# Moving one addition from VectorE to GpSimd, five transposes to a later place, and two sums ahead of two transfers, in a two-way cross-attention kernel

## The chip, the cores and the metric

The kernel runs on one core of a Trainium2 chip. The metric is the device time of one execution in microseconds (us); three executions of the kernel before gave 942.03, 942.37 and 944.33 us, with a median of 942.37. Engines are named as in the profile: PE is TensorE (PEld its weight loads), DVE is VectorE, ACT is ScalarE, POOL is GpSimd, SP is the queue that starts most transfers. "L12" is line 12 of the kernel before.

## The reference, cut to what matters

All arrays are float32. There are B = 16 batches of S = 100 query rows of width H = 640, and a context of 722 tokens of width 384 for each batch. The last 4 tokens (`ca`) are split off; the other 718 (`enc`) are keys and values of an ordinary attention with 8 heads of width 80. The 4 tokens feed a second attention, whose queries come out of a third one over the rows of `x`. Both results are added and projected:

```python
hs = _mha(hidden_states @ Wq, enc @ Wk, enc @ Wv)
ca_q1 = jnp.einsum('btc,th->bch', ca, Wq_ca)[:, indices, :]
ca_q2 = _mha(ca_q1, residual, residual) @ Wq
ca_hs2 = _mha(ca_q2, ca @ Wk_ca, ca @ Wv_ca)
out = (hs + ca_hs2) @ Wout + b_out + residual
```

## The kernel before, in words

A preparation of about 60 us loads and combines weights and makes the keys and values of batch 0. Then a Python loop over the 16 batches `b` issues everything in an order that is written out by hand: each engine runs its own queue in exactly the order of the code, and engines wait for each other through semaphores only where data or buffers demand it. No scheduler moves anything in the loop.

One step of the loop, for the batches 1 to 14, goes like this:

- `scores` (L623): three groups of score matmuls for batch b; ACT copies them to `st[0..2]`, and DVE keeps a running maximum `most` (L1229). `Maximum` turns that into one maximum for each row, `top.over`, through two 32x32 transposes on DVE (L675, L705) and reductions.
- `Values` (L443) makes the values of batch b, and `Keys` (L474) the keys of batch b+1, by a fast matrix multiplication that needs 15 products each. A product accumulates in a PSUM bank (A to E) which is read several times, between products: by ACT the first time that a block of the result is touched (L416), by DVE as an addition later (L414). So PE may write a bank again only when the reading before it has ended. `vv.go(n)` and `kk.go(n)` issue the next n products; `both(n)` does both. Banks C, D and E come from a pool of two PSUM buffers (`psum1`), keys' A and B from another of two (`psumk`).
- Among these products stand `subtract(i)` on DVE (L1217, `st[i]` minus the maximum) and `exponential(i)` on ACT (L1225).
- The second attention is computed by element-wise work: `second.scores1` for batch b+1 (POOL, L784 and L791), `now.scores2` and `now.softmax3` for batch b (small DVE work; L862 makes the weights `p`), and `now.values2` (POOL, L876 products and L883 sums), which writes `hs2`. Its four input rows `vb` are transfers: two of them started from POOL's own queue by `load` (L833), two from SP.
- `last_keys` (L568) makes the last 128 columns of the keys of batch b+1. After odd batches `queries` (L544) makes the queries of the next two batches.
- The values are applied to the probabilities (L1409), and DVE writes `hs` (L1423). For all batches but 0, DVE also adds `hs2` there (L1430). In batch 0, `hs2` is not ready by then, and the addition is done later, in batch 1's step.
- `last` is the batch before. `last.transpose()` transposes its `hs` in five pieces of 128 columns on PE (L931) into one PSUM tile `hst_ps`, and ACT copies them to `hsT` (L944). In the batches from 2 on this stands at the start of the step.
- The output projection takes chunks of 128 rows. Ten of the thirteen chunks are done in five pairs (`PAIRS`, in the steps b = 3, 6, 8, 11 and 13) by `project_pair` (L1010), which saves products by using sums of the two chunks. `last.sums()` makes the first two sums on POOL (L991): `sum1`, and a new first part of `two = hsT[r+1]`. `project_pair` begins with five matmuls that need neither (b1 and b2), then come two that need the second sum and the combined weight `wout2`. POOL's own steps between are L1027, L1030 and L1031; L1030 overwrites what the two matmuls read, and L1031 makes the weight for a later product.

In batch 1's step before the change, the late addition (L1315) stands on DVE between four readings of PSUM banks and `top.go()` (L705), and the transposes of batch 0 stand among the products, into a `psum1` buffer.

Of the kernel before, what the change touches and what calls it, by code (L numbers as in the profile page):

```python
# [10 lines left out]
ALU = mybir.AluOpType  # L11
# [3 lines left out]
B, S, H = 16, 100, 640  # L15
# [4 lines left out]
HC = H // P  # L20
# [18 lines left out]
PAIRS = {ENDS[r + 1]: r for r in range(0, 10, 2)}  # L39
# [96 lines left out]
def kernel(  # L136
# [18 lines left out]
    nc = tc.nc  # L155
# [21 lines left out]
    def psumk(name):  # L177
        return psk.tile([P, 512], F32, tag="psk", name=name)
# [24 lines left out]
    def hsT_tile(name):  # L203
        return main.tile([P, HC, P], F32, tag="hsT", name=name, bufs=3)
# [19 lines left out]
    def rest_tile(name):  # L224
        return main.tile([P, len(A_REST), KT], F32, tag="rest", name=name)

    def load_enc(b):
        enc = enc_tile(f"enc_{b}"), None
        for u, lo, hi in ((0, 0, 3), (1, 1, 3), (2, 0, 2)):
            at = A_RAW[u, lo]  # L230
            nc.sync.dma_start(
                out=enc[0][:, at : at + hi - lo],
                in_=enct[b][:, lo:hi, u * (KT - 1) : u * (KT - 1) + KT],
            )
        return enc

    def load_rest(b, enc):
        if b == 1:
            room = hsT_tile("rest_1").rearrange("p c s -> p (c s)")
            rest = room[:, : len(A_REST) * KT].rearrange("p (i k) -> p i k", k=KT)  # L240
        else:
            rest = rest_tile(f"rest_{b}")
        for (u, c), i in A_REST.items():
            nc.sync.dma_start(
                out=rest[:, i], in_=enct[b][:, c, u * (KT - 1) : u * (KT - 1) + KT]
            )
        return enc[0], rest
# [459 lines left out]
    def load_m(b):  # L707
        if b < 2:
            return lambda c: m_sb[c][:, b * HT : (b + 1) * HT]
        mb = small.tile([P, HC, HT], F32, tag="mb", name=f"mb_{b}", bufs=2)  # L710
        nc.sync.dma_start(
            out=mb, in_=m_d[:, :, b * HT : (b + 1) * HT].rearrange("c p n -> p c n")
        )
        return lambda c: mb[:, c]
# [182 lines left out]
    class Last:  # L897
# [23 lines left out]
                return [(0, slice(0, H))]  # L921
            return [(64 * k, slice(k * (H // 2), (k + 1) * (H // 2))) for k in range(2)]

        def transpose(self, chunks=[(0, HC)], get=psumk):
            b, hs = self.b, self.hs
            if not self.t_ps:
                self.t_ps = get(f"hst_ps_{b}")
            t_v = self.t_ps[:, : HC * S].rearrange("p (c s) -> p c s", c=HC)
            for c0, c1 in chunks:
                for c in range(c0, c1):  # L930
                    nc.tensor.transpose(  # L931
                        t_v[:, c], hs[:S, c * P : (c + 1) * P], ident[:S, :S]
                    )
                for r, (lo, n) in enumerate(OC):
                    first, end = max(lo, b * S), min(lo + n, (b + 1) * S)
                    if first >= end:
                        continue
                    if r not in hsTs:
                        hsTs[r] = (
                            spare[0].rearrange("p (c s) -> p c s", c=HC)  # L940
                            if r == len(OC) - 1
                            else hsT_tile(f"hsT_{r}")
                        )
                    nc.scalar.copy(  # L944
                        hsTs[r][:, c0:c1, first - lo : end - lo],
                        t_v[:, c0:c1, first - b * S : end - b * S],
                    )
# [238 lines left out]
    last, enc_next, second_next = None, load_rest(1, load_enc(1)), Second(1, xT)  # L1186
# [8 lines left out]
    for b in range(B):  # L1195
# [28 lines left out]
        def exponential(i):  # L1224
            nc.scalar.activation(st[i], st[i], AF.Exp, scale=SCALE)  # L1225
# [29 lines left out]
        if b == 0:  # L1255
            second.scores1()
            m_next = load_m(b + 2)
            kk.go(3)
            top.go(3)
            first_values(3, e_in, (act, act), get=bank)  # L1260
            top.go(1)
            kk.go(2)
            now.scores2()
            first_values(0, e_in, (act, act), (0,), bank)
            top.go()
            kk.go(3)
            first_values(0, e_in, (act, act), (1,), bank)
            now.softmax3()
            kk.go(2)
            subtract(0)  # L1270
            exponential(0)
            kk.go(2)
            subtract(1)
            kk.go(3)
            exponential(1)
            second_next, enc_next = loads()
            less = subtract(2)
            exponential(2)
            last_keys(b + 1, enc)
            enc_next = load_rest(b + 2, enc_next)  # L1280
            keys(m_next)
            now.values2(less)
            enc_sums(enc_next)
            second.softmax1(4)
        elif b + 1 < B:
            if b > 1:
                last.transpose()
            vv = Values(b, e_in)

            def both(n):  # L1290
                vv.go(n)
                kk.go(n)

            forms = [wout_sb[:, 2 * i : 2 * i + 2, k * (H // 2) : (k + 1) * (H // 2)]
                     for i in range(2) for k in range(2)]
            if b == 2:
                for o, left, right in (
                    (forms[1], forms[1], forms[0]),
                    (wout2[:, 0], forms[3], forms[1]),
                    (wout2[:, 1], forms[2], wout2[:, 0]),  # L1300
                ):
                    nc.gpsimd.tensor_tensor(o, left, right, ALU.subtract)
            elif last.b - 1 in PAIRS:
                nc.gpsimd.tensor_tensor(wout2[:, 0], wout2[:, 0], forms[0], ALU.add)
            second.scores1(seen)
            if b == 1:
                now.load()
            last.load()
            top.go(3)
            both(3)  # L1310
            now.scores2()
            top.go(1)
            both(2)
            if b == 1:
                nc.vector.tensor_tensor(last.hs[:S], last.hs[:S], last.hs2, ALU.add)  # L1315
            top.go()
            both(2)
            if b == 1:
                last.transpose(get=psum1)
            both(1)  # L1320
            now.softmax3()
            now.values2()
            vv.go(2)
            kk.go(1)
            subtract(0)
            exponential(0)
            vv.go(1)
            subtract(1)
            vv.go(1)
            kk.go(2)  # L1330
            exponential(1)
            vv.go(1)
            kk.go(2)
            both(1)
            both(1)
            if b == 1:
                for f in list(wv_there):
                    nc.scalar.copy(wv_sb[:, W_AT[f]], wv_there.pop(f))
            second.load()
            if b == 1:  # L1340
                nc.gpsimd.dma_start(out=bias, in_=bout[0].partition_broadcast(P))
            second_next, enc_next = loads()
            if b + 2 < B:
                m_next = load_m(b + 2)
            subtract(2)
            exponential(2)
            last_keys(b + 1, enc)
            if b + 2 < B:
                enc_next = load_rest(b + 2, enc_next)
            if last.b in PAIRS:  # L1350
                last.sums()
                second.softmax1(3)
                last.project_pair()
                if last.b == max(PAIRS):
                    nc.sync.dma_start(
                        out=forms[1],
                        in_=wout[: 2 * P, H // 2 :].rearrange("(c p) n -> p c n", p=P),
                    )
            second.softmax1()
        else:  # L1360
            room = enc_tile("spare").rearrange("p f k -> p (f k)")
            spare.extend(room[:, i * H : (i + 1) * H] for i in range(2))
            last.transpose()
            vv = Values(b, e_in)
            last.load()
            mine.load()
            top.go(3)
            vv.go(3)
            last.project_few(len(OC) - 2)
            now.scores2()  # L1370
            top.go(1)
            vv.go(2)
            top.go()
            vv.go(3)
            now.softmax3()
            now.values2()
            vv.go(2)
            subtract(0)
            exponential(0)
            vv.go(5)  # L1380
            for i in (1, 2):
                subtract(i)
                exponential(i)
            last.project()
# [47 lines left out]
        last = mine  # L1432
# [55 lines left out]
```

## Time and profile before

| | |
|---|---|
| median of three runs | 942.37 us |
| the profiled execution | 941.78 us, of which the span on the core is 940.1 us |
| PE busy | 931.7 us (99%) |
| DVE busy | 687.0 us (73%) |
| POOL busy | 669.3 us (71%) |
| ACT busy | 372.9 us (40%) |
| granted TensorE clock | 1.0 throughout |
| step of batch 1, from its scores to its last values | about 99 to 157 us |
| the five pair projections begin at | 248, 421, 536, 700 and 816 us |

The profiled execution's time is 1.68 us more than its span, and 0.59 us less than the median. "Busy" counts the time of instructions on an engine; times in a timeline are from the span's start. In a timeline a line gives the start, the time, the engine, the line and operation, what is written from what, how many instructions are merged, and in square brackets the idle time before with what ended it.

### The profile page before, as it was taken

The page shows a single profiled execution, that of the slowest core. Times are in us where ns is not written, and L with a number is a line of the kernel's source. Part 1 is how long each engine was busy: PE and PEld are TensorE (multiplying, and loading weights), DVE is VectorE, ACT ScalarE, POOL GpSimd, SP SyncE. Part 2 cuts the span into 40 slices and gives each one's busy share as a digit, 9 for nine tenths or more (in the row PEclk, how much of TensorE's full clock was granted, in tenths as well). Part 3 has the DMA queues.
Part 4 walks back from the last instruction along what each step waited for, and adds up shares of the span by engine and source line. Part 5 has one row for each costly group of instructions (what it writes and reads, how often), then busy time and mean ns, then how long its engine had stood idle before and what let it go on. Part 6 is the DMA issues. An engine that isn't in the chain of part 4 may idle for free.

```text
span 940.1 us, 25799 instructions
## 1 busy us (share of the span) xinstructions
PE 931.7 (99%) x11195; PEld 792.4 (84%) x11195; DVE 687.0 (73%) x1099; ACT 372.9 (40%) x615; POOL 669.3 (71%) x613
## 2 busy tenths in 40 slices
PE   9999999999999999999999999999999999999998
PEld 6998879797797979888798787988879888798866
DVE  3859793989739796684967859579782897738884
ACT  1244443434324343442434434244441534415341
POOL 5657988679937878496784968758795587956713
PEclk9999999999999999999999999999999999999999
DMA  8732022050300304031030400205030050310201
GB/s 257 248 108 73 19 75 66 6 148 2 102 31 16 111 5 126 2 105 50 24 107 3 124 31 30 74 2 152 2 102 30 1 152 2 102 44 2 81 17 43
DMA packets 49672, 62.82 MB, mean 67 GB/s; under 512 B 14072, under 2 KB 38200, under 8 KB 49560
## 3 DMA queue, kind: packets, MB, share of 16 engines
q1 hardware_dynamic: 45512, 51.49, 18.0%
q0 software_dynamic: 3024, 8.53, 3.0%
q8 instruction: 88, 1.44, 0.6%
q10 hardware_dynamic: 1024, 1.15, 0.4%
q14 instruction: 24, 0.20, 0.1%
HBM read 55.59 MB, written 5.57 MB: 65 GB/s over the span
## 4 chain that ended last, share of the span: by engine, by line
PE 87%; POOL 6%; DVE 4%; issue 1%; ACT 1%; DMA 0%; DVEq 0%; POOLq 0%
PE a_ps L1409 12%; PE s_ps L623 12%; PE v_psA L443 9%; PE v_psB L443 7%; PE q_ps L544 7%; PE kT_ps L568 7%; PE k_psA L474 6%; PE k_psB L474 5%; PE o_ps L1010 5%; PE v_psC L443 3%; PE k_psC L474 2%; POOL hs L876 2%; PE v_ps L384 2%; PE y_ps L749 2%; DVE most L1229 1%; PE v_psD L443 1%
## 5 line engine op out<-in xcount | busy, mean ns | idle before, releaser
L784 POOL TENSOR_TENSOR e<-ca,g 100x800 f32<-100x800 f32 x64 | 99.9, 1571 | 135.6 <-DVE most L1229 126.6
L876 POOL TENSOR_TENSOR hs<-vb,p 100x640 f32<-100x640 f32 x64 | 119.6, 1877 | 52.5 <-DVE p L862 41.2
L509 POOL TENSOR_TENSOR enc<-enc 128x240 f32<-128x240 f32 x135 | 106.9, 801 | 21.5 <-DMA enc<-in_enct 14.4
L1409 PEld LDWEIGHTS a_ps<-vs,st 120*36 120x36 f32 (+3 forms) x3072 | 109.2, 125 | 4.9 <-issue 4.8
L1409 PE MATMUL a_ps<-vs,st 120*36 120x81 f32 (+3 forms) x3072 | 112.0, 233 | 0.0
L443 PE MATMUL v_psA<-wv_sb,enc 128*120 128x320 f32 x352 | 109.5, 434 | 0.0
L1217 DVE TENSOR_TENSOR st<-st,over 120x1600 f32<-120x1600 f32 x48 | 103.3, 2154 | 0.0
L883 POOL TENSOR_TENSOR hs<-hs,hs 100x640 f32<-100x640 f32 x48 | 100.5, 2095 | 3.8
L623 PE MATMUL s_ps<-qp,kT 32*120 32x100 f32 x3072 | 98.8, 263 | 0.0
L623 PEld LDWEIGHTS s_ps<-qp,kT 32*120 32x120 f32 x3072 | 95.8, 179 | 1.8 <-issue 0.4
L791 POOL TENSOR_TENSOR e<-e,e 100x800 f32<-100x800 f32 x48 | 90.6, 1887 | 3.8
L443 PE MATMUL v_psB<-wv_sb,enc 128*120 128x320 f32 x296 | 91.9, 433 | 0.0
L640 ACT COPY st<-s_ps 120x800 f32<-120x800 f32 x64 | 49.7, 828 | 100.5 <-PE s_ps L623 100.5
L474 PE MATMUL k_psA<-enc,wk_sb 128*128 128x240 f32 x360 | 87.6, 366 | 0.0
L1229 DVE TENSOR_TENSOR most<-most,st 120x800 f32<-120x800 f32 x64 | 68.5, 1070 | 23.6 <-ACT st L634 22.5
L1225 ACT ACTIVATE st<-st 120x1600 f32<-120x1600 f32 x48 | 73.8, 1538 | 23.6 <-DVE st L1217 23.5
L474 PEld LDWEIGHTS k_psA<-enc,wk_sb 128*128 128x128 f32 x360 | 68.3, 190 | 16.7
L443 PEld LDWEIGHTS v_psA<-wv_sb,enc 128*120 128x120 f32 x352 | 63.2, 183 | 22.6 <-issue 0.5
L474 PE MATMUL k_psB<-enc,wk_sb 128*128 128x240 f32 x300 | 73.1, 366 | 0.1
L443 PEld LDWEIGHTS v_psB<-wv_sb,enc 128*120 128x120 f32 x296 | 54.0, 183 | 21.9 <-DVE vs L414 0.4
L544 PE MATMUL q_ps<-xT,wq_sb 128*128 128x200 f32 x400 | 69.1, 333 | 0.0
L544 PEld LDWEIGHTS q_ps<-xT,wq_sb 128*128 128x128 f32 x400 | 67.9, 190 | 1.1 <-issue 0.5
(162 smaller groups left out, 1729.1 us busy)
## 6 DMA issues: line engine op xcount, KB each, us to landing
vb<-va_d POOLq DMA_DIRECT2D x32, 250.0 KB, 4.1
vb<-va_d SPq DMA_DIRECT2D x32, 250.0 KB
enc<-in_enct SPq DMA_DIRECT2D x30, 240.0 KB
enc<-in_enct SPq DMA_DIRECT2D x15, 360.0 KB
xT<-in_xt SPq DMA_DIRECT2D x8, 500.0 KB
rest<-in_enct SPq DMA_DIRECT2D x31, 120.0 KB
xn<-in_x SPq DMA_DIRECT2D x11, 320.0 KB
out<-xn SPq DMA_DIRECT2D x11, 320.0 KB
```

The lines of the kernel that those rows point to most:

```text
L443: nc.tensor.matmul(at[0][j][:KN, : H // 2], a_form(self.enc, f)[:, j * KN : (j + 1) * KN], wv_there.get(f, wv_sb[:, W_AT[f]]), start=first ...
L474: nc.tensor.matmul(at[:, i * KT : (i + 1) * KT], wk_sb[:, W_AT[f], i], a_form(self.enc, f), start=(first and i == 0), stop=last, skip_grou ...
L509: nc.gpsimd.tensor_tensor(out, left, right, op)
L544: nc.tensor.matmul(q_ps[:, : 2 * S].rearrange("p (j s) -> p j s", j=2), wq_sb[:, c, n * P : (n + 1) * P], xT[:, :, c, :], start=(c == 0), ...
L623: nc.tensor.matmul(s_ps[r][:n, 256 * a + lo : 256 * a + hi], kT[rows, c, u, j * KN : (j + 1) * KN], rhs, start=(a == 0 and c == 0), stop=( ...
L784: first = nc.gpsimd.tensor_tensor(to, self.ca[:, t, :].unsqueeze(1).to_broadcast([S, NH, S]), g[:, :, t].unsqueeze(2).to_broadcast([S, NH, ...
L791: nc.gpsimd.tensor_tensor(e, e, to, ALU.add)
L876: first = nc.gpsimd.tensor_tensor(to, self.vb[t][:S].rearrange("p (h d) -> p h d", h=NH), p2[:, :, t].unsqueeze(2).to_broadcast([S, NH, D] ...
L883: nc.gpsimd.tensor_tensor(sums, sums, to, ALU.add)
L1217: return nc.vector.tensor_tensor(st[i], st[i], top.over[:KN].unsqueeze(1).to_broadcast([KN, 2, ROWS]), ALU.subtract,)
L1229: most_now = nc.vector.tensor_tensor(most[:KN], most[:KN], st[i][:, u], ALU.max)
L1409: nc.tensor.matmul(a_v[lo:hi, h % 4], st[i // 2][: KEYS[i], i % 2, h * S + lo : h * S + hi], block(i, h // 4)[: KEYS[i], h % 4], start=(i ...
```

## The change

1. The late addition of batch 0's `hs` and `hs2` leaves DVE. It goes to POOL, behind `softmax3` and ahead of `values2` of batch 1; on POOL's queue that is behind the two `vb` transfers of batch 1 (L833) and ahead of L876.
2. Batch 0's transposes go from the middle of batch 1's products to the place behind `last_keys`, ahead of the queries of batches 2 and 3, and their PSUM tile comes from `psumk` and not from `psum1`. ACT's copy of them moves likewise, behind the two copies of the last keys (L579).
3. In the five steps with a pair, `last.sums()` (POOL, L991) goes from behind the next batch's two `vb` transfers (`second.load()`, L833) and the other loads to the place right behind `values2`, ahead of them.

```diff
-        def transpose(self, chunks=[(0, HC)], get=psumk):
+        def transpose(self, chunks=[(0, HC)]):
             b, hs = self.b, self.hs
             if not self.t_ps:
-                self.t_ps = get(f"hst_ps_{b}")
+                self.t_ps = psumk(f"hst_ps_{b}")
...
             top.go(1)
             both(2)
-            if b == 1:
-                nc.vector.tensor_tensor(last.hs[:S], last.hs[:S], last.hs2, ALU.add)
             top.go()
             both(2)
-            if b == 1:
-                last.transpose(get=psum1)
             both(1)
             now.softmax3()
+            if b == 1:
+                nc.gpsimd.tensor_tensor(last.hs[:S], last.hs[:S], last.hs2, ALU.add)
             now.values2()
+            if last.b in PAIRS:
+                last.sums()
             vv.go(2)
             kk.go(1)
             subtract(0)
...
             last_keys(b + 1, enc)
             if b + 2 < B:
                 enc_next = load_rest(b + 2, enc_next)
+            if b == 1:
+                last.transpose()
             if last.b in PAIRS:
-                last.sums()
                 second.softmax1(3)
                 last.project_pair()
```

No instruction is added or dropped; one changes its engine.

## The prediction

> **What bounds the kernel now.** I read the engine totals first, then the table of waits for PE, then the timelines around the places that change.
>
> ```profile
> PE 931.7 (99%) x11195; PEld 792.4 (84%) x11195; DVE 687.0 (73%) x1099; ACT 372.9 (40%) x615; POOL 669.3 (71%) x613
> ```
>
> PE is at work in 931.7 of 940.1 us. What can be won is what PE waits for, and the table of waits names two items that the change touches (total us, times, longest):
>
> ```profile
> PE k_psE L474 <- DVE vs L414: 1.6, 2, 1.3
> ...
> PEld o_ps L1010 <- POOL hsT L991: 2.9, 5, 0.8
> ```
>
> The first is almost all one wait in batch 1's step; its timeline:
>
> ```profile
> 117.39 1.24 PE L443 MATMUL v_psE<-wv_sb,enc 128*120 128x320 f32 x4
> 119.27 1.19 DVE L1315 TENSOR_TENSOR hs<-hs,hs 100x640 f32<-100x640 f32 x1
> 119.55 0.97 PE L474 MATMUL k_psA<-enc,wk_sb 128*128 128x240 f32 x4
> 119.86 2.00 POOL L784 TENSOR_TENSOR e<-ca,g 100x800 f32<-100x800 f32 x1
> 120.38 1.00 DVE L705 STREAM_TRANSPOSE over<-spread 128x800 f32<-128x800 f32 x1
> 121.31 0.84 DVE L414 TENSOR_TENSOR vs<-v_psE,vs 120x320 f32<-120x320 f32 x2
> 121.81 1.08 PE L474 MATMUL k_psE<-enc,wk_sb 128*128 128x240 f32 x4 [1.29 <-DVE vs L414]
> 125.52 1.87 POOL L791 TENSOR_TENSOR e<-e,e 100x800 f32<-100x800 f32 x1
> 126.28 1.16 DVE L862 TENSOR_TENSOR p<-e,sm 100x32 f32<-100x32 f32 x1
> 127.37 1.81 DVE L1217 TENSOR_TENSOR st<-st,over 120x1600 f32<-120x1600 f32 x1
> 129.90 1.81 DVE L1217 TENSOR_TENSOR st<-st,over 120x1600 f32<-120x1600 f32 x1
> 131.16 2.91 POOL L876 TENSOR_TENSOR hs<-vb,p 100x640 f32<-100x640 f32 x2 [2.72 <-DMA vb<-va_d]
> 132.37 0.64 DVE L414 TENSOR_TENSOR kT<-k_psC,kT 128x480 f32<-128x480 f32 x1
> 133.68 0.97 PE L474 MATMUL k_psC<-enc,wk_sb 128*128 128x240 f32 x4
> ```
>
> Four key matmuls take 0.81 us from start to start, so `k_psE` was due at 119.55 + 0.81 = 120.36 and came 1.45 late, behind DVE's reading of `v_psE`. The addition L1315 stands ahead of that reading. To be seen too: DVE is busy nearly without a gap, so it sets the pace here.
>
> The second item, in the first of the five pairs:
>
> ```profile
> 248.14 2.86 PE L1010 MATMUL o_ps<-wout_sb,hsT 128*128 128x320 f32 x10
> 248.56 1.10 POOL L833 DMA_DIRECT2D vb<-va_d  x2
> 249.67 0.74 POOL L991 TENSOR_TENSOR sum<-hsT 128x256 f32<-128x256 f32 x1
> 250.49 0.72 POOL L991 TENSOR_TENSOR hsT<-sum,hsT 128x256 f32<-128x256 f32 x1
> 251.27 2.42 PE L1010 MATMUL o_ps<-wout,hsT 128*128 128x320 f32 x8 [0.27 <-POOL hsT L991]
> 251.29 0.73 POOL L1027 TENSOR_TENSOR hsT<-hsT,hsT 128x256 f32<-128x256 f32 x1
> 252.76 0.73 POOL L1030 TENSOR_TENSOR hsT<-hsT 128x256 f32<-128x256 f32 x1 [0.74 <-PE o_ps L1010]
> ```
>
> POOL issues two transfers in 1.10 us while PE runs its ten free instructions; the sums come after, and PE waits.
>
> **The five pairs.** Ten instructions at 0.27 us take 2.70, so the next was due at 250.84 and came at 251.27: 0.43 late. The other four pairs start the same two groups at 420.54 and 423.38, 535.80 and 538.61, 700.09 and 702.94, 815.60 and 818.58: late by 0.14, 0.11, 0.15 and 0.28. The sum is 1.11. After each wait the next eight instructions take 2.26 and not 8 x 0.27 = 2.16, the cost of a weight load that nothing covers: 5 x 0.10 = 0.50. Together 1.6 us.
>
> Put ahead of the transfers, the second sum ends 1.10 earlier, at 250.1; PE's load asks at about 250.64. So all 1.6 us go. What is late next is L1031, which PE's load already awaits 0.24 us without PE losing any. It follows L1030, which waits for PE and so moves along. L1027 doesn't move, since POOL has the same work ahead of it; its end at 252.02 allows L1030 0.67 earlier, and 0.53 are asked for. The other pairs ask for 0.2 to 0.4 out of 0.66 to 0.67. The transfers start 1.5 us later, land 4.1 us on, and are read first at 299.87 in this trace: some 45 us of cover. The sums' inputs, ACT's copies L944 early in the step, are long there.
>
> **Batch 1: the addition leaves DVE.** DVE's next instruction came 1.11 us after L1315's start, so the reading of `v_psE` comes 1.11 earlier and `k_psE` starts at 120.70, still 0.34 late. (The other `k_psE` wait, in batch 3, is 0.28.) The transposes leave this place too: from 122.72 to the next product at 123.15, 0.43. PE is then 1.54 ahead and would reach the second `k_psC` product at 132.14. But that overwrites a bank that DVE reads until 133.01, so DVE decides.
>
> DVE and POOL do not run freely beside each other. L862 takes 0.19 us in its shortest case and 1.16 here: it ends at 127.44, when POOL's L791 ends (127.39). L1315 took 1.19 while POOL's L791 ended at 119.77, and POOL's L784 behind it took 2.00 and not 1.54. I read this as turns: a DVE instruction with both inputs in SBUF and a POOL addition exclude each other.
>
> So, step by step. Without L1315, L784 is back to 1.54 and POOL's L791 ends 0.46 earlier, at 126.93. L862 still runs into it; the first L1217 starts and ends 0.46 earlier and frees DVE at 128.64. POOL's new addition stands behind two transfer issues of 1.10 together, is ready at 128.03, and must wait for that L1217. Its turn then takes 1.49 (of L883's 3.02 at 137.51, that much is left when the L1217 before it has ended). The second L1217 is ready at 129.44 and must wait. The nearest row for this is batch 6, where POOL's L876 with a turn of 1.21 sits between the two: the second L1217 lasts 2.09 from 408.49, so it got its turn 1.08 after its predecessor's end. With 0.28 more that is 128.64 + 1.36 = 130.0, where it was 129.90. Hence DVE's reading of `k_psC` ends 0.12 later than before, at 133.13, and PE goes on at 133.18, where it was 133.68: 0.50 ahead, less 0.10 for the bare weight load. The transposes' 0.43 come back at the new place. Batch 1 gives 0.0 us: a wait behind DVE is traded for another.
>
> Bounds: if the addition never stands in DVE's way, the whole 1.11 is won. If L862 doesn't come earlier although the addition pushes the second L1217, 0.46 are lost. I take 0, by batch 6's row, which is the nearest.
>
> [...]
>
> **What is moved along.** The transposes now wait for POOL's sum, ready near 130; PE comes there near 141.7, 11 us later. Without that cover 50 query matmuls would queue behind them. ACT's copy (0.58) stands ahead of the query copies, where ACT idles 0.87; the query tile that takes that PSUM buffer is third, 3.4 us of matmuls on. `psum1` has one tile fewer between `k_psE` and `v_psC`: `v_psC`'s second half now needs DVE's reading of `k_psE`, done near 123.3, and asks at 123.85. POOL's `values2` stands behind the addition: its wait of 2.72 for the transfer covers it but for 0.1 to 0.3; SP's two `vb` transfers behind L876 shift as much, and SP's next loads wait for PE anyway. POOL's next deadline has 7.31 us of idle ahead of it (L784 at 169.06). All nothing.
>
> **Sum.** The profiled execution is 941.78 us (span 940.1, 1.68 around it): 941.78 - 1.6 - 0.0 = 940.2. The median is 0.59 above the profiled one: 942.37 - 1.6 = 940.8.
>
> **Rivals.**
> *A: batch 1's wait is won too.* Either POOL's addition gets its turn when DVE reads PSUM, or the second L1217 is not delayed. For it: several margins here are 0.1 us. Against it: batch 3, where L1217 pairs with L876 like in batch 6, has a wait at this very product (0.51 on the load). Price: 942.37 - 1.6 - 1.1 = 939.7.
> *B: the wait returns at L1030 and L1031.* L1027 stays behind the transfer issues. If those take longer in their new place, POOL and not PE times L1030. It decides at 0.67 us more than the 1.10: from there a pair wins nothing. With 1.0 more each pair loses 0.33 against before, 5 x 0.33 = 1.6: 944.0, slower. Against it: the 32 issues of this kind last 537 to 622 ns, so two differ by at most 0.14 from 1.10.
> [...]
>
> **How the numbers follow.** About 0.3% (2.8 us) is what a measurement of this kernel tells from no change. My forecast, the pairs alone (about 940.0 to 941.2 with the bounds of batch 1 short of A), has 0.60; A 0.25; B 0.08; 0.07 is left for shifts that I don't see. Faster than 939.5 are 0.4 of A, a tenth of the forecast and a little of the rest: 0.18. Slower than 945.2 are a fifth of B and half the rest: 0.05. Within: 0.77. The range goes from below A, 939.0, to 943.0, above the forecast's worst (0.46 lost, 941.2) by the spread of the runs shown.
>
> **What would show it.** Right: PE's wait for L991 is gone in all five pairs, and the eight instructions take 2.16; in batch 1 `k_psE` waits about 0.2, a new wait of `k_psC` for DVE's L414 near 132 takes about 1 us, and the second L1217 or POOL's addition is long. Wrong: no such `k_psC` wait (A), or longer waits for L1031 (B); a loss or gain outside batch 1 and the pair steps would refute the whole account.

## The result, and the profile after

| | before | after |
|---|---|---|
| median (lowest to highest) of 8 runs each, us | 942.43 (941.59 to 944.33) | 940.02 (938.97 to 941.14) |
| ratio of the two, 95% interval | | 0.9974 [0.9964, 0.9985] |
| profiled execution, us | 941.78 | 940.45 |
| its span, us | 940.1 | 938.7 |

The kernel is 2.4 us faster (1.4 to 3.4 by the interval), just inside the 0.3% that the prediction set as its bound (the author's estimate: no run shows that limit, and the interval of these 0.26% leaves out a ratio of 1). The forecast was 940.8, with a range of 939.0 to 943.0. The time falls within it, but between the forecast and rival A (939.7), and the traces show that rival A's wait was won. The range held because it reached down to rival A, and not because batch 1 went as the forecast said.

The engine totals after; PE again fills the whole span:

```profile
PE 929.9 (99%) x11195; PEld 792.8 (84%) x11195; DVE 687.9 (73%) x1098; ACT 372.6 (40%) x615; POOL 671.8 (72%) x614
```

From the table of all waits after (who waits, for whom: total us, times, longest). The item of 2.9 us for L991 is gone, `k_psE` has fallen from 1.6 to 0.2, and L1031 holds PE's load for the same 1.2 us as before, so PE loses nothing new there:

```profile
POOL hsT L1030 <- PE o_ps L1010: 2.8, 5, 0.7
...
PEld o_ps L1010 <- POOL wout L1031: 1.2, 5, 0.2
...
PE k_psE L474 <- DVE vs L414: 0.2, 1, 0.2
```

The first pair after, POOL and PE. The sums now stand ahead of the transfer issues, and the ten free instructions run into the eight without a wait. The eight take 2.16 (249.86 to 252.02), and POOL, not PE, does the waiting at L1030:

```profile
247.17 2.85 PE L1010 MATMUL o_ps<-wout_sb,hsT 128*128 128x320 f32 x10
...
248.43 0.73 POOL L991 TENSOR_TENSOR hsT<-sum,hsT 128x256 f32<-128x256 f32 x1
249.10 1.10 POOL L833 DMA_DIRECT2D vb<-va_d  x2
249.86 2.32 PE L1010 MATMUL o_ps<-wout,hsT 128*128 128x320 f32 x8
...
251.25 0.72 POOL L1030 TENSOR_TENSOR hsT<-hsT 128x256 f32<-128x256 f32 x1 [0.30 <-PE o_ps L1010]
252.02 0.70 PE L1010 MATMUL o_ps<-wout_sb,hsT 128*128 128x320 f32 x2
```

Batch 1 after. Its product `v_psE` starts at 118.21 and not at 117.39, so the trace is 0.82 us later here than that of before; subtract that to compare:

```profile
121.53 1.08 PE L474 MATMUL k_psE<-enc,wk_sb 128*128 128x240 f32 x4 [0.19 <-DVE vs L414]
...
125.86 0.19 DVE L862 TENSOR_TENSOR p<-e,sm 100x32 f32<-100x32 f32 x1
125.87 3.66 POOL L791 TENSOR_TENSOR e<-e,e 100x800 f32<-100x800 f32 x1
125.96 1.82 DVE L1217 TENSOR_TENSOR st<-st,over 120x1600 f32<-120x1600 f32 x1
...
128.97 2.24 DVE L1217 TENSOR_TENSOR st<-st,over 120x1600 f32<-120x1600 f32 x1
...
130.59 2.04 POOL L1319 TENSOR_TENSOR hs<-hs,hs 100x640 f32<-100x640 f32 x1
...
131.87 0.64 DVE L414 TENSOR_TENSOR kT<-k_psC,kT 128x480 f32<-128x480 f32 x1
132.95 0.97 PE L474 MATMUL k_psC<-enc,wk_sb 128*128 128x240 f32 x4
```

Two things are to be seen. L862 takes 0.19 and not 1.16, and now it is POOL's L791 that is long, 3.66 and not 1.87. And the second `k_psC` product carries no wait: DVE's reading ends at 132.51, 0.44 ahead of it. Most of the wait for `k_psE` was won and nothing took its place. (L1319 is the moved addition.)

Below, "batch 1's stretch" is the time from the `v_psE` product of batch 1 to that of batch 2. It is 58.86 us before and 57.76 after, 1.10 less. It holds parts 1 and 2 of the change and no pair.

### The profile page after: what moved, and what is told of

The parts are those of the page before. It is cut to its first block, busy times and chain, and to the rows that moved or that the text cites. A ratio compares the mean times of both kernels' runs of the same rounds, so it can differ in the third digit from the quotient of the medians.

```text
span 938.7 us, 25800 instructions
## 1 busy us (share of the span) xinstructions
PE 929.9 (99%) x11195; PEld 792.8 (84%) x11195; DVE 687.9 (73%) x1098; ACT 372.6 (40%) x615; POOL 671.8 (72%) x614
## 3 DMA queue, kind: packets, MB, share of 16 engines
q10 hardware_dynamic: 1024, 1.15, 0.4%
## 4 chain that ended last, share of the span: by engine, by line
PE 96%; DVE 2%; issue 1%; DMA 1%; ACT 0%; POOL 0%; ACTq 0%; DVEq 0%
PE s_ps L623 12%; PE a_ps L1410 12%; PE v_psA L443 10%; PE v_psB L443 8%; PE kT_ps L568 8%; PE k_psA L474 7%; PE q_ps L544 7%; PE k_psB L474 6%; PE o_ps L1010 5%; PE v_psC L443 3%; PE k_psC L474 3%; PE y_ps L749 2%; PE v_ps L384 2%; PE v_psD L443 2%; PE v_psE L443 2%; PE k_psE L474 1%
## 5 line engine op out<-in xcount | busy, mean ns | idle before, releaser
L784 POOL TENSOR_TENSOR e<-ca,g 100x800 f32<-100x800 f32 x64 | 99.5, 1565 | 137.2 <-DVE most L1229 123.6
L876 POOL TENSOR_TENSOR hs<-vb,p 100x640 f32<-100x640 f32 x64 | 120.5, 1892 | 50.4 <-DVE p L862 41.2
L509 POOL TENSOR_TENSOR enc<-enc 128x240 f32<-128x240 f32 x135 | 104.5, 783 | 20.0 <-DMA enc<-in_enct 12.9
L1217 DVE TENSOR_TENSOR st<-st,over 120x1600 f32<-120x1600 f32 x48 | 104.4, 2177 | 0.0
L791 POOL TENSOR_TENSOR e<-e,e 100x800 f32<-100x800 f32 x48 | 92.3, 1923 | 3.8
```

Source lines behind the costliest of these rows:

```text
L509: nc.gpsimd.tensor_tensor(out, left, right, op)
L784: first = nc.gpsimd.tensor_tensor(to, self.ca[:, t, :].unsqueeze(1).to_broadcast([S, NH, S]), g[:, :, t].unsqueeze(2).to_broadcast([S, NH, ...
L791: nc.gpsimd.tensor_tensor(e, e, to, ALU.add)
L876: first = nc.gpsimd.tensor_tensor(to, self.vb[t][:S].rearrange("p (h d) -> p h d", h=NH), p2[:, :, t].unsqueeze(2).to_broadcast([S, NH, D] ...
L1217: return nc.vector.tensor_tensor(st[i], st[i], top.over[:KN].unsqueeze(1).to_broadcast([KN, 2, ROWS]), ALU.subtract,)
```

## The experiments

The first four share one chip and 33 runs of the kernel before (median 942.63), the other four another chip and 16 runs (942.26). The two medians are 0.37 apart, so ratios are compared. A diff against the kernel after is marked so.

**The sums alone** (the kernel before with part 3 only):

```diff
             now.values2()
+            if last.b in PAIRS:
+                last.sums()
             vv.go(2)
...
             if last.b in PAIRS:
-                last.sums()
                 second.softmax1(3)
```

> Only the third part: the sums L991 go ahead of the two transfers; the addition stays on DVE and the transposes stay in the middle. Theory (the parts add up: five pairs 1.6 us, batch 1 its own 1.1): no wait of PE for L991 in any pair, each pair shorter by 0.54, 0.25, 0.22, 0.26 and 0.39 us, batch 1 as before with k_psE 1.45 late; time 942.4 - 1.6 = 940.8. Rival (the whole gain is the pairs, and batch 1 gives nothing): 940.0, like the changed kernel.

Measured: 940.86 us, ratio 0.9982 [0.9973, 0.9991], that is 1.77 us less. Its table of waits has no item for L991, and the wait of batch 1 stands as before:

```profile
PE k_psE L474 <- DVE vs L414: 1.3, 1, 1.3
```

The pairs' 1.6 us are real, and batch 1's stretch is unchanged (difference 0.00).

**Parts 1 and 2 alone** (against the kernel after):

```diff
             now.values2()
-            if last.b in PAIRS:
-                last.sums()
...
             if last.b in PAIRS:
+                last.sums()
                 second.softmax1(3)
```

> Only the first two parts: addition on POOL, transposes behind the last keys; the sums stay behind the transfers. Theory: the stretch from v_psE in batch 1 to the same in batch 2 is 1.1 us shorter than before, the pairs wait for L991 as before; time 942.4 - 1.1 = 941.3. Rival by the prediction's sum: a wait of the second k_psC product of about 1 us in batch 1, and 942.4.

Measured: 941.56 us, ratio 0.9993 [0.9984, 1.0002]. The time alone can't be told from no change. The trace can: batch 1's stretch is 1.09 shorter, the pairs wait as before, and the long instruction of DVE and POOL has changed sides as in the kernel after. The table of waits, then the timeline:

```profile
PEld o_ps L1010 <- POOL hsT L991: 2.7, 5, 0.8
```

```profile
127.13 0.19 DVE L862 TENSOR_TENSOR p<-e,sm 100x32 f32<-100x32 f32 x1
127.15 3.65 POOL L791 TENSOR_TENSOR e<-e,e 100x800 f32<-100x800 f32 x1
```

The parts by themselves make 1.77 + 1.07 = 2.84 us, against 2.4 for the whole change. The intervals are about 1 us either way, so the times agree with parts that add up, but don't prove it.

**The turn lost** (against the kernel after; two more reductions of the same data in batch 1 make DVE come to L862 later):

```diff
-            nc.vector.tensor_reduce(sm, e, AX.X, ALU.add)
+            for _ in range(3 if b == 1 else 1):
+                nc.vector.tensor_reduce(sm, e, AX.X, ALU.add)
```

> The changed kernel, and in batch 1 two more DVE reductions (the same result again, some 0.2 us each) ahead of L862. Theory (which of DVE's L862 and POOL's last L791 gets its turn first decides, and it was a matter of 0.01 us): L862 now comes 0.4 later, POOL's L791 goes first and lasts 1.9 us, L862 ends with it, the first L1217 starts about 1.7 us later than in the changed kernel, and the second k_psC product waits for DVE for about 1 us; batch 1's stretch is about 1.0 us longer, time 941.0. Rival (only DVE's work counts, 0.4 us, which its slack at that product takes up): no wait at k_psC, batch 1 within 0.2 us of the changed kernel, 940.0.

Measured: 941.38 us, ratio 0.9986 [0.9977, 0.9994]; batch 1's stretch is 1.15 longer than after, as long as before (+0.05). The three reductions last 0.62 together, so the two added ones are some 0.4 of it; the loss is larger than what was put in. The timeline (lines below L859 are one higher than in the kernel after):

```profile
125.27 1.88 POOL L791 TENSOR_TENSOR e<-e,e 100x800 f32<-100x800 f32 x1
125.67 1.53 DVE L863 TENSOR_TENSOR p<-e,sm 100x32 f32<-100x32 f32 x1
...
128.20 2.15 POOL L1320 TENSOR_TENSOR hs<-hs,hs 100x640 f32<-100x640 f32 x1
129.66 2.38 DVE L1218 TENSOR_TENSOR st<-st,over 120x1600 f32<-120x1600 f32 x1
...
133.39 1.08 PE L474 MATMUL k_psC<-enc,wk_sb 128*128 128x240 f32 x4 [0.90 <-DVE kT L414]
```

This is the chain that the prediction wrote for batch 1, once POOL gets its turn first: L791 is short and the weights long, POOL's addition comes between the two subtractions and pushes the second, and `k_psC` waits. Less this trace's offset of 0.21, PE goes on at 133.18, the very time that the prediction worked out. So the chain was right, and what it started from, POOL's turn ahead of DVE's L862, was not.

**Four transfers for two** (against the kernel after; rival B's mechanism: the two `vb` rows that POOL starts in a pair's step go as halves, so that the issues take longer):

```diff
-            engine.dma_start(
-                out=vb[:S], in_=va_d[b * T + t].unsqueeze(0).to_broadcast([S, H])
-            )
+            halves = 2 if engine is nc.gpsimd and b - 2 in PAIRS else 1
+            for k in range(halves):
+                w = H // halves
+                cols = slice(k * w, (k + 1) * w)
+                engine.dma_start(
+                    out=vb[:S, cols],
+                    in_=va_d[b * T + t][cols].unsqueeze(0).to_broadcast([S, w]),
+                )
```

> The changed kernel, with the two transfers ahead of L1027 in the pair steps cut in halves: four issues, about 2.2 us and not 1.1. Theory (rival B's place is real, POOL has 0.30 to 0.67 us of idle ahead of L1030): L1030 and L1031 come 0.4 to 0.8 us later, PE waits for L1031 in each pair by as much, in all about 2.7 us; time 942.7. Rival (PE's wait for L1031 has cover of its own): 940.0.

Measured: 942.96 us, ratio 0.9999 [0.9990, 1.0007]; the pairs' gain is gone (each is now longer than before), and batch 1's stretch keeps its 1.11. The first pair's timeline (lines behind L833 are five higher):

```profile
250.00 2.17 POOL L837 DMA_DIRECT2D vb<-va_d  x4
...
252.99 0.73 POOL L1035 TENSOR_TENSOR hsT<-hsT 128x256 f32<-128x256 f32 x1
...
255.27 1.34 PE L1015 MATMUL o_ps<-wout,hsT 128*128 128x320 f32 x4 [0.56 <-POOL wout L1036]
```

POOL no longer waits for PE at L1030 (here L1035), and PE waits for L1031 (here L1036, 1.54 from 253.68) instead, 2.0 us in the five pairs. Rival B's place is real; its mechanism did not occur, since the two issues after take 1.10, as before.

**The transposes stay, the addition goes** (against the kernel after):

```diff
...
             top.go()
             both(2)
-            both(1)
-            now.softmax3()
             if b == 1:
                 nc.gpsimd.tensor_tensor(last.hs[:S], last.hs[:S], last.hs2, ALU.add)
+                last.transpose(get=psum1)
+            both(1)
+            now.softmax3()
...
-            if b == 1:
-                last.transpose()
```

> The changed kernel, but the transposes stay where they were, among the products of batch 1 (the addition on POOL and the sums ahead of the transfers as changed). Theory (the two moves of batch 1 need each other): PE reaches the transposes near 122.4 and waits for POOL's addition, which stands behind L791 and two transfer issues and ends near 130.4; 8 us lost in batch 1, time 948. Rival (most of it is given back, as DVE and ACT use the pause to catch up and PE had waits coming): below 944.

Measured: 949.95 us, ratio 1.0077 [1.0063, 1.0091]: slower than before by 7.7, and batch 1's stretch is 10.72 longer than after. PE waits 7.78 for POOL's addition, which stands behind L791 and two issues. The timeline:

```profile
128.45 1.54 POOL L1317 TENSOR_TENSOR hs<-hs,hs 100x640 f32<-100x640 f32 x1
130.04 1.10 PE L931 MATMUL hst_ps<-ident,hs 100*128 100x100 f32 x5 [7.78 <-POOL hs L1317]
130.93 2.38 PE L443 MATMUL v_psB<-wv_sb,enc 128*120 128x320 f32 x4
```

The wait explains 7.8 of the 10.7. The rest shows in the table by stretches of the same kernel (stretch; its length; busy us and instructions of PE, PEld, DVE, ACT and POOL; granted clock; DMA share; GB/s):

```profile
122.20:130.00 7.80, 0.07 (x1) 0.00 (x0) 1.49 (x3) 0.00 (x0) 7.62 (x6) 0.73 0.15 40
130.00:132.00 2.00, 1.96 (x7) 1.57 (x8) 0.00 (x0) 0.57 (x1) 0.00 (x0) 0.50 0.25 101
...
134.00:136.00 2.00, 2.00 (x6) 1.44 (x5) 1.12 (x4) 0.00 (x0) 0.00 (x0) 0.50 0.00 0
136.00:138.00 2.00, 2.00 (x9) 1.47 (x9) 1.93 (x2) 1.15 (x3) 1.64 (x1) 1.00 0.03 8
```

PE's clock fell to 0.50 during the wait and stayed there for 6 us of work: four values matmuls take 2.17 from start to start (130.93 to 133.10) where they take 1.08 elsewhere. So 6 us of PE time do the work of 3, and 7.8 + 3.0 accounts for the 10.7. Part 1 pays only together with part 2.

**The transposes go, the addition stays** (against the kernel after):

```diff
             both(2)
+            if b == 1:
+                nc.vector.tensor_tensor(last.hs[:S], last.hs[:S], last.hs2, ALU.add)
             top.go()
...
-            if b == 1:
-                nc.gpsimd.tensor_tensor(last.hs[:S], last.hs[:S], last.hs2, ALU.add)
```

> The changed kernel, but the addition stays on DVE where it was (the transposes behind the last keys and the sums ahead of the transfers as changed). Theory (all of batch 1's gain is the 1.1 us that the addition takes of DVE): k_psE comes 1.45 late as before, the transposes' 0.43 only change their place, batch 1's stretch is as before within 0.1 us; time 940.9, like the sums alone. Rival (taking the transposes out of the products gives something by itself): stretch shorter by 0.4 us or more.

Measured: 940.84 us, ratio 0.9986 [0.9977, 0.9994]; batch 1's stretch is that of before (+0.05). Moving the transposes alone gives nothing: the two kernels with the addition on DVE and the pairs' sums moved have 0.9982 and 0.9986. The timeline has the old wait, and L862 loses its turn again:

```profile
121.79 1.08 PE L474 MATMUL k_psE<-enc,wk_sb 128*128 128x240 f32 x4 [1.33 <-DVE vs L414]
...
126.05 1.36 DVE L862 TENSOR_TENSOR p<-e,sm 100x32 f32<-100x32 f32 x1
```

**No addition at all** (against the kernel after; batch 0's rows go on without the second attention):

```diff
-            if b == 1:
-                nc.gpsimd.tensor_tensor(last.hs[:S], last.hs[:S], last.hs2, ALU.add)
```

> The changed kernel without the addition of batch 0's two attentions (left out altogether). Theory (POOL's addition costs nothing, since L862 and the first L1217 get their turn before it and POOL's wait for the transfers covers it): batch 1's stretch as in the changed kernel within 0.1 us; time 940.0. Rival (the addition still holds up the second L1217, and so PE): stretch shorter by 0.2 to 0.5 us.

Measured: 939.21 us, ratio 0.9975 [0.9961, 0.9989], against 0.9974 after; batch 1's stretch is 0.89 shorter than before, no better than after's 1.10. The addition on POOL costs nothing there. The timeline shows the same turn (L862 at 125.82 with 0.19), and a second subtraction of the same 2.24, so it was not POOL's addition that lengthened it. (L791, which ends at 129.50 here and 129.53 after, overlaps it in both.)

```profile
125.83 3.67 POOL L791 TENSOR_TENSOR e<-e,e 100x800 f32<-100x800 f32 x1
...
128.94 2.24 DVE L1217 TENSOR_TENSOR st<-st,over 120x1600 f32<-120x1600 f32 x1
```

**The maximum later** (against the kernel after; an attempt to win the rest of `k_psE`'s wait):

```diff
-            top.go()
+            if b != 1:
+                top.go()
             both(2)
+            if b == 1:
+                top.go()
```

> The changed kernel, and in batch 1 the second transpose of the maximum (L705, 1.0 us on DVE) is issued behind the next two products' readings and not ahead of them. Theory (the rest of k_psE's wait, 0.36 and 0.10 for the bare weight load, is DVE's L705 ahead of the reading of v_psE): no wait of k_psE, batch 1's stretch 0.4 us shorter than in the changed kernel; time 939.6. Rival (DVE's work is the same, so PE waits for it later, at k_psC): stretch as in the changed kernel, 940.0.

Measured: 939.41 us, ratio 0.9966 [0.9953, 0.9978], which can't be told from after's 0.9974 [0.9964, 0.9985]. The stretch is 0.19 shorter than after. `k_psE` no longer waits, but the second `k_psC` product now does:

```profile
132.41 0.70 PEld L474 LDWEIGHTS k_psC<-enc,wk_sb 128*128 128x128 f32 x4 [0.36 <-DVE kT L414]
```

Part of what this wins is given back. No kernel here is shown to beat the one after.

## Why the prediction was right, and where it failed

**The pairs: right.** The forecast was 1.6 us; the sums alone gave 1.77. By its own terms 0.43 + 0.10 = 0.53 was due in the first pair, where 248.14 to 258.37 before has become 247.17 to 256.86 after, 0.54 less. For the other four the terms are 0.24, 0.21, 0.25 and 0.38; the steps with these pairs are 0.26, 0.23, 0.26 and 0.39 shorter. L1031 costs PE nothing, as foretold. POOL waits between 0.30 and 0.67 at L1030, so the room was larger than foretold; it was put at 0.67 - 0.53 = 0.14 in the first pair, which has the 0.30. For rival B the price was 0.33 against before for each pair with 1.0 us more of issues; with four issues, 1.07 more, the steps with the second to fifth pair are 0.31, 0.33, 0.27 and 0.54 longer than before.

**Batch 1: the step that failed is "L862 still runs into it".** Up to there the chain held: L784 is back to 1.54, and `k_psE` starts at 121.53 - 0.82 = 120.71, where 120.70 was written. But with L1315 gone DVE also came to L862 sooner. The prediction moved POOL's L791 by its 0.46, to 125.06, but did not ask where its own 1.11 put L862: at 126.28 - 1.11 = 125.17, only 0.11 behind. In the trace L862 came 1.24 sooner (125.86 - 0.82 = 125.04), started 0.01 us ahead of L791 and had the turn. The first L1217 then started at 125.96 - 0.82 = 125.14, 2.23 ahead of before, where the prediction gave it 0.46. The second came 1.75 earlier and DVE's reading of `k_psC` ended 1.32 earlier, not 0.12 later. PE took the product at 132.95 - 0.82 = 132.13; the prediction had said that PE could reach it at 132.14 if DVE did not decide. So the 0.0 became 1.1, rival A's price, and no wait of `k_psC` came, which was the prediction's own sign for A. A's first reason did occur: the addition L1319 ends at 132.63, and it takes 1.54 where nothing holds it up, so its turn began at about 131.1, when the second L1217 ended (131.21) and DVE went on to reading PSUM. But what put it there was L862's turn, which neither of A's reasons names; and without the addition the second L1217 takes the same 2.24. The subtractions came early enough. The kernel with the turn lost shows the other end of the same fork: stretch as before, PE on at the foretold time.

The same fork decides L791's length: 3.65 to 3.67 in the five kernels where DVE was ahead (after, parts 1 and 2 alone, four transfers, no addition, the maximum later), and L862's 1.16 to 1.53 where it was not (before, the sums alone, the turn lost, the addition staying on DVE). In the five, L862 started 0.01 to 0.03 us ahead of L791; in the four it started 0.40 to 0.76 behind. Where between these the outcome changes was not measured. Each kernel has one trace, so how often the turn goes one way or the other for one kernel is open. The medians agree with the traces: 0.9974, 0.9975 and 0.9966 where the sums have moved and the turn is won, 0.9982 and 0.9986 where they have moved and the addition is on DVE, 0.9986 where the turn is lost.

That DVE and POOL take turns is read from these lengths: L791's 3.66 for 1.88 where DVE was ahead, and L862's 1.16 to 1.53 for 0.19 where it was not. DVE's readings of PSUM show nothing of it: in the trace of before, L791 from 117.89 takes 1.88, and the L414 of 117.95 beside it 0.65, the median of each. What makes the two take turns, no run shows. The prediction's 0.0 for batch 1 came out with the turn lost (+0.05), and not with the turn won (1.10 shorter).

**What the single profile hides.** The profiled span fell by 1.4 only, although its parts say more. Batch 1 (1.10), the first pair's stretch of the loop (1.24) and the other pairs (0.26 + 0.23 + 0.26 + 0.39 = 1.14) make 3.5. Against that, the trace of after starts batch 1 0.82 late, of which 0.57 arises in the preparation, where PE waits 1.0 us for the DMA of `wv_sb`, and it has three waits of PE (0.60, 0.52 and 0.22, 1.34 together) that name no releaser and that the trace of before doesn't have at these places. The first two:

```profile
657.68 0.35 PE L623 MATMUL s_ps<-qp,kT 32*120 32x100 f32 x3 [0.60 <-issue]
665.46 0.39 PE L811 MATMUL z_ps<-y_sb,e 100*32 100x33 f32 x22 [0.52 <-issue]
```

They come and go: the sums alone, four transfers, the addition staying and no addition have neither of the first two, and the turn lost and the maximum later have the second (0.51 and 0.52). That is why the medians over several runs, and not two spans, decide. In the 1.24, 0.54 is the pair; most of the other 0.7 is the wait of PE for `k_psE` in batch 3's step, which the trace of before has (0.28, and 0.66 on the weight load) and that of after has not; the weight load for `k_psC` there waits 0.37 and not 0.51. The same stretch is 1.34 shorter with the sums alone, 0.99 with the turn lost and 0.56 with four transfers, so this varies from trace to trace. By the prediction's last sign such gains and losses outside batch 1 and the pairs would refute its account. The waits do not follow the three parts of the change, since four transfers has all three and neither of the first two, and the medians agree with the two gains alone; but the prediction did not foresee them, and their cause stays open.

## What to carry to other kernels

Where one engine is busy for 99% of the time, a few waits are all there is to win, and putting short instructions ahead of transfer issues on a queue (1.1 us for two) won them all here, since the next wait had room for it; read that room first. When work moves between DVE and POOL, and the traces show their instructions lengthened beside each other (here L862 to 1.16 from 0.19), write out their turns instruction by instruction and price both outcomes of each close one: here a lead of 0.01 us won 1.1 us, and a lag of 0.40 lost it. A move that adds a wait needs the consumer moved with it, past the producer's queue: one half of such a pair of moves without the other cost 10.7 us in its stretch.

## What was not expected of the hardware

- POOL's addition L791, which started 0.01 us behind L862 (0.19 us), did not get its turn when L862 ended. DVE's next instruction, L1217 (1.82), started 0.10 after L862 and ended at 127.78, and L791 ended 1.75 after that, at 129.53. So L791 took 3.66 and not 1.88, which reads as a wait for both. The prediction had no case in which one engine goes twice while the other waits.
- One wait of PE, of 7.78 us, cost more than its length. In the kernel whose transposes stayed, the clock fell to 0.50 some 3.5 us into that wait (at about 125.7) and came back at 136.0, 6 us after PE went on; that cost 3 us. In the other kernels no wait of PE in batch 1 was longer than 1.33, and the clock was 1.00 (from 99 to 158 us before and after, from 122.2 to 138 in the rest). Whether a wait between these two lengths does the same, and what brings the clock back, was not measured.
